# Message passing over 128 small graphs: blocks 2 to 14 ranked by edge count, a heavy and a light graph sharing nine slot tiles

## The chip, the core and the metric

One core of a Trainium2 chip runs the whole kernel. It has five engines that the profile names: PE (matrix products), DVE and ACT (vector and scalar work), POOL (vector work, and the queue that can issue indirect transfers) and SP (whose queue issues nearly all other transfers). Each works through its own queue in order; they wait for one another by semaphores. The metric is the device time in microseconds, the median of several runs.

## The reference

There are B = 128 graphs of N = 64 nodes with C = 128 features, in `x` (128, 64, 128), and a symmetric 0/1 matrix `adj` (128, 64, 64) with ones on the diagonal. The reference computes, for every ordered pair (i, j) of nodes of a graph, a message by a three-layer perceptron, keeps the messages whose `adj[i, j]` is 1, sums them over j, and feeds node i and its sum to a second perceptron:

```python
f_i, f_j = x[:, :, None, :], x[:, None, :, :]            # both broadcast to (B, P, P, C)
messages = mlp(concat(f_i, f_j), msg_*)                   # relu, layernorm, relu, layernorm, linear
agg      = sum(messages * adj[..., None], axis=2)
updated  = x + mlp(concat(x, agg), upd_*)
```

with `mlp` = linear, ReLU, layer normalization, linear, ReLU, layer normalization, linear. The adjacency is random: with the reference's seed a graph has 498 to 622 ones, 552 on average, of 4096.

## The kernel before, in words

Only the edges are computed. An edge gets a **slot**; a graph has CAP = 640 slots, which is five tiles of 128 (`TG = 5`). Two graphs make a **pair** (64 nodes on partitions 0 to 63, 64 on 64 to 127), four pairs a **block** of eight graphs, 16 blocks in all. All tiles are laid end to end and cut in **chunks** of four tiles (512 slots): 640 tiles, 160 chunks, ten a block. Weights that depend only on parameters are derived at the start.

For each block, `load_adj` and `load_x` bring the adjacency and the features (tiles `an`, `xn`), `rank` counts each node's edges along its row (`rk`), `count` sums the counts over nodes by a product with a triangular matrix (`lt`), `place` and `place_out` give every edge its slot number (`posall`), and `rows`, `rows_hi` and `rows_lo` make the first layer's two products for every node, split in a high and a low part (`abh`, `abl`).

For each pair, `distance` and `make_tp` (ACT, DVE) mark which slots belong to which node i (`tp`, 640 columns); `node_rows` casts it on POOL (`i`), `marks` and `compare` (PE, DVE) find node j of each slot (`j`), and `stack` puts both one above the other by four transfers on SP's queue into the 0/1 matrix `s`. `node_marks` turns `tp` by a transposing transfer (`oh`) for the sum at the end.

For each chunk, `gather` (L933) multiplies `s` by `abl` and `abh` into the PSUM bank `hps`, in pieces that end at a graph's border; `relu0` (ACT, L938) gives `h`; `turn_h` (PE, L943) transposes it four times for `stats0` (DVE, L629), the first normalization's sums. `layer1` (PE, L986) multiplies each of the four tiles by `w1c` into bank `z`. The bias, scaled by the deviation, is added in one of two ways, chosen by `by_vector`: for half of the chunks POOL makes it (`seed_all`, `u`, L973) and DVE adds it with the ReLU (L613); for the others ACT writes it into the bank first (`seed`, L980) and applies the ReLU (L997). `stats1` (DVE, L629) sums up the result `y`. For a group of five chunks `var1_step`, `root1_of` and `inverse_of` give the factors `m_q`; `weights` (POOL, L1029) multiplies them with `oh`, and `reduce` (PE, L1044) sums the slots of each node, after which a `Unit` runs the second perceptron for the block and `finish` stores 512 rows of the output.

The order is written by hand: `at(n, tag, fn, ...)` gives each step a time, 144 units a chunk plus a correction from the table `WHEN`, and a sort by these times is the order in which every engine's queue is filled. Nothing reorders it later. If a graph does not fit its slots, a flag sends all graphs through a dense path behind.

Of the kernel before, what the change touches and what calls it, by code (L numbers as in the profile page):

```python
# [25 lines left out]
    "<lambda>.3": {100: 398},  # L26
    "<lambda>.4": {100: 795},
    "<lambda>.6": {100: 4632},
    "<lambda>.7": {100: 284},
    "ahead.0": {100: 233},  # L30
    "ahead.1": {100: 132},
    "ahead.10": {100: 11},
    "ahead.11": {100: -1},
    "ahead.2": {100: 50},
    "ahead.5": {100: 113},
    "ahead.8": {100: 157},
    "ahead.9": {100: 215},
    "bias0": {3: -1471, 112: -1906, 113: -1642, 114: -17},
    "bias0_0": {115: 1153},
    "bias0_2": {115: 525},  # L40
    "bounds": {100: -15375},
# [8 lines left out]
    "count": {8: -190, 101: 140, 102: 122, 115: -186},  # L50
    "count.0": {100: 47},
    "count_out": {9: -228, 101: -2, 102: 190, 115: -239},
    "count_out.0": {100: 63},
    "degrees": {9: -358, 101: -137, 102: 105, 115: -608},
    "degrees.0": {100: -699},
    "distance": {0: -539, 3: 150, 5: -495, 8: -349, 103: 84, 104: 283, 105: -140, 106: 202,
        107: -511, 108: 189, 158: -852, 159: -528, 160: -749, 161: -525, 162: -737, 163: -1005},
    "distance.0": {100: 181},
    "distance.1": {101: 189},
    "distance.2": {102: 311},  # L60
    "empties.0": {100: 111},
    "empties.1": {100: 152},
    "empties.10": {100: 200},
    "empties.11": {100: 169},
    "empties.2": {100: -14},
    "empties.3": {100: 100},
    "empties.4": {100: 111},
    "empties.5": {100: 55},
    "empties.6": {100: -50},
    "empties.7": {100: -92},  # L70
    "empties.8": {100: -22},
    "empties.9": {100: 128},
    "finish": {8: 220, 110: 217, 111: 771, 112: 335, 113: -14, 114: 4865},
    "finish_0": {115: 6154},
    "finish_2": {115: 6519},
    "flag_in": {100: 118},
    "flag_max": {100: 160},
    "flag_out": {100: 377},
    "flag_sum": {100: 514},
    "flag_turn": {100: 45},  # L80
# [295 lines left out]
def tile_gnn(  # L376
# [9 lines left out]
    uw2: bass.AP, ub2: bass.AP,  # L386
    out: bass.AP,
):

# [1255 lines left out]
```

## Time and profile before

| what | value |
|---|---|
| median of the runs | 498.48 us (497.48 to 499.75, three runs) |
| profiled execution, first to last instruction | 497.9 us, no time of its own beside this span |
| PE, PEld busy | 486.0 us, 461.3 us |
| DVE busy | 465.2 us |
| ACT busy | 397.3 us |
| POOL busy | 348.4 us |
| SP's transfers, share of the 16 DMA engines | 55.9%, 62.36 MB |

The time of an execution is that of its slowest core, here the only one. A group's mean duration of a PE instruction is not its share of the engine's time, since the next one starts before it ends; the steps from start to start are in the timeline.

### The profile page before, as it was taken

Reading aid. Unit: us, or ns where it says so; the run is one execution under the profiler, and the core shown is the slowest. Engines: PE = TensorE matmul, PEld = TensorE weight load, DVE = VectorE, ACT = ScalarE, POOL = GpSimd, SP = SyncE. Lnnn points to the kernel's source line nnn. Section 1 sums busy time; section 2 is a strip of 40 time slices with the busy share of each in tenths; the row PEclk is TensorE's granted clock in tenths of the full one; section 3 lists DMA queues with packets and bytes.
Section 4 is the critical chain, followed back from the end, with each engine's and each line's share of the span. In section 5 each row is a group of like instructions: output and inputs, shape, how many; then the busy total and the mean of one; then the engine's idle time right before and its main releaser. Section 6 shows DMA issues by size and latency. Waiting matters only on the chain. (4 is left out here: it accounts for less than half of the span.)

```text
span 497.9 us, 15949 instructions
## 1 busy us (share of the span) xinstructions
PE 486.0 (98%) x5947; PEld 461.3 (93%) x5947; DVE 465.2 (93%) x1225; ACT 397.3 (80%) x907; POOL 348.4 (70%) x563
## 2 busy tenths in 40 slices
PE   7999999999999999999999999999999999999995
PEld 5889999999999999999899999999999999999994
DVE  7999999999999999999999999999999988989985
ACT  6999978878787887878778786888878778867754
POOL 3285776967959676795867859676696859565770
PEclk9999999999999999999999999999999999999998
DMA  4766836367574656854465574656655448625331
GB/s 122 148 145 157 182 99 150 93 167 152 126 140 110 126 142 150 168 122 118 117 143 143 126 153 103 132 128 158 152 123 128 101 112 165 152 74 129 66 34 47
DMA packets 91474, 63.55 MB, mean 128 GB/s; under 512 B 57473, under 2 KB 75522, under 8 KB 91394
## 3 DMA queue, kind: packets, MB, share of 16 engines
q1 hardware_dynamic: 91106, 62.36, 55.9%
q8 instruction: 49, 0.80, 0.7%
q14 instruction: 31, 0.25, 0.2%
q10 hardware_dynamic: 288, 0.13, 0.1%
HBM read 7.15 MB, written 4.19 MB: 23 GB/s over the span
## 5 line engine op out<-in xcount | busy, mean ns | idle before, releaser
L986 PE MATMUL z<-w1c,h 128*128 128x128 f32 x1280 | 190.0, 275 | 0.0
L986 PEld LDWEIGHTS z<-w1c,h 128*128 128x128 f32 x1280 | 172.4, 192 | 4.0 <-DVE uy_st L629 0.2
L938 ACT ACTIVATE h<-hps,b0c 128x512 f32<-128x512 f32 x160 | 109.0, 682 | 36.0 <-PE hps L933 35.5
L629 DVE BATCH_NORM_STATS2 st<-hT 128x6 f32<-128x256 f32 x320 | 122.9, 417 | 7.1 <-PE hT L943 4.8
L629 DVE BATCH_NORM_STATS2 st<-y 128x6 f32<-128x256 f32 x320 | 127.1, 419 | 0.5 <-ACT y L997 0.3
L980 ACT ACTIVATE z<-b1b,m_sd 128x128 f32<-128x128 f32 x320 | 117.3, 368 | 9.2 <-DVE y L613 3.6
L943 PE MATMUL hT<-ident,h 128*128 128x128 f32 x640 | 112.9, 276 | 0.3 <-DVE st L629 0.2
L933 PE MATMUL hps<-s,abl 128*128 128x512 f32 (+3 forms) x256 | 96.6, 380 | 2.6 <-ACT h L938 2.1
L933 PE MATMUL hps<-s,abh 128*128 128x512 f32 (+3 forms) x256 | 89.8, 358 | 0.0
L973 POOL TENSOR_TENSOR u<-b1b,m_sd 128x512 f32<-128x512 f32 x80 | 83.7, 1049 | 7.6 <-ACT m_sd L637 7.6
L943 PEld LDWEIGHTS hT<-ident,h 128*128 128x128 f32 x640 | 76.3, 141 | 3.4 <-issue 1.2
L1029 POOL TENSOR_TENSOR w<-oh,m_q 128x192 f32<-128x192 f16 x126 | 62.1, 514 | 9.4 <-DVE m_q L658 3.1
L916 DVE TENSOR_TENSOR j<-mk,cmpt 128x320 fp32r<-128x320 f32 x124 | 59.4, 479 | 6.3 <-PE mk L908 3.9
L891 POOL CAST i<-tp 128x640 fp32r<-128x640 f16 x58 | 41.8, 720 | 29.3 <-DMA s<-i 27.7
L997 ACT ACTIVATE y<-z 128x512 f32<-128x512 f32 x80 | 47.4, 595 | 17.8 <-PE z L986 17.5
L613 DVE CUSTOM_DVE_ANT_0 y<-z,u 128x512 f32<-128x512 f32 x80 | 54.1, 676 | 4.0 <-PE z L986 3.7
L933 PEld LDWEIGHTS hps<-s,abl 128*128 128x128 f32 x256 | 48.8, 191 | 8.0 <-ACT h L938 3.7
L876 ACT ACTIVATE d<-slot,mid 128x640 f16<-128x640 f16 x64 | 52.1, 818 | 1.7 <-POOL mid L765 1.0
L647 POOL TENSOR_TENSOR m_v<-m_v,st 128x20 f32<-128x20 f32 x31 | 7.3, 234 | 60.9 <-DVE st L629 59.6
L933 PEld LDWEIGHTS hps<-s,abh 128*128 128x128 f32 x256 | 49.1, 192 | 0.2
L1044 PE MATMUL ys<-y,w 128*32 128x128 f32 x1488 | 44.1, 274 | 0.0
L1044 PEld LDWEIGHTS ys<-y,w 128*32 128x32 f32 x1488 | 39.6, 110 | 2.5 <-issue 2.1
(193 smaller groups left out, 887.9 us busy)
## 6 DMA issues: line engine op xcount, KB each, us to landing
s<-i SPq DMA_DIRECT2D x124, 160.0 KB, 3.0
s<-j SPq DMA_DIRECT2D x124, 160.0 KB, 2.8
xn<-in_x_dram SPq DMA_DIRECT2D x15, 256.0 KB, 3.9
out_dram<-uo SPq DMA_DIRECT2D x15, 256.0 KB, 2.5
an<-in_adj_dram SPq DMA_DIRECT2D x16, 128.0 KB, 3.5
oh<-tp SPq DMA_TRANSPOSE x64, 3.0
xn<-in_x_dram SPq DMA_DIRECT2D x2, 128.0 KB, 3.0
out_dram<-uo SPq DMA_DIRECT2D x2, 128.0 KB, 3.4
```

The lines of the kernel that those rows point to most:

```text
L613: nc.vector._custom_dve(TENSOR_ADD_SAT, out=o, in0=ps, in1=sb, s0=BIG, s1=0.0)
L629: nc.vector.bn_stats(st, src.rearrange("p t c -> p c t"))
L876: nc.scalar.activation(D[p], slot.rearrange("p (t e) -> p t e", e=P), AF.Abs, bias=blocks[b]["mid"][:, q:q + 1], scale=-1.0)
L916: nc.vector.tensor_tensor(JR[p][:, c], MK.pop((p, k))[:, 0:HC], cmpt[:, c], op=ALU.is_equal)
L933: nc.tensor.matmul(HP[n][:, c:c + w], lhsT=blocks[g // (2 * PB)]["ab", g // 4 % 2][k][:, g % 4, :], rhs=S[g // 2][:, g % 2, e:e + w], star ...
L938: nc.scalar.activation(H[n], HP.pop(n), AF.Relu, bias=b0c)
L943: nc.tensor.transpose(HT[n][:, t, :], H[n][:, t * P:(t + 1) * P], ident)
L973: nc.gpsimd.tensor_tensor(U[n], bc(W["b1b"], CH), SR[q][:, k:k + CH].unsqueeze(2).to_broadcast([P, CH, C]), op=ALU.mult)
L980: nc.scalar.activation(z_of(n)[:, t, :], W["b1b"], AF.Copy, scale=SR[q][:, k:k + 1])
L986: nc.tensor.matmul(ps[:, t, :], lhsT=H[n][:, t * P:(t + 1) * P], rhs=W["w1c"], start=by_vector(n) and t == 0, stop=True, skip_group_check= ...
L1029: (nc.vector if p == NP - 2 else nc.gpsimd).tensor_tensor(WT[p][:, g], oh, qs, op=ALU.mult)
L1044: nc.tensor.matmul(YS[b][g * N + m * HN:g * N + (m + 1) * HN, k, :], lhsT=w[:, g, m, u, :], rhs=y, start=(u == 0), stop=(u == TH - 1), til ...
```

## The change

Blocks 0, 1 and 15 stay as they are. In blocks 2 to 14 (104 graphs) a pair gets nine tiles in place of ten. The pair's first graph fills slots from the front, the second from the back (`lts`, `lth` and `side` take the place of `lt` in `count`, `count_out` and `whole`), and they share the middle tile: the first may use slots 0 to 639 of 1152, the second 576 to 1151, and both are gathered into columns 576 to 639. A node's upper half still starts at slot 256 or later, counted from the graph's own end. So a block has nine chunks, and the program 147 chunks in place of 160, in 588 tiles in place of 640. The columns gathered for a pair fall from 1280 to 1216; everything that works on a pair's 640-column marks, on the block or on the second perceptron keeps its size. Of the nine chunks four go by POOL and DVE and five by ACT (before, five and five). The flag's test is extended by two columns for the new borders.

Which graphs meet is found on the chip. `all_adj` loads the 104 adjacency matrices once more, a graph a partition, by eight transfers of 104 x 512; `edges` adds the eight on POOL; `sort_keys` to `sort_out` rank the sums with a handful of DVE instructions and two products, and place the graph of rank r at position 2r or at the mirrored odd position, so that the heaviest meets the lightest. The list `idx` holds for each block of the 128 partitions' rows in `x`, `adj` and the output (a graph is 16 rows).

With it each of the 13 blocks is moved by way of memory: `fetch` gathers the adjacency (128 rows of 1 KB) and later the features (128 rows of 2 KB) by an indirect transfer on POOL's queue into `stg` (two buffers), `put` writes them to a scratch `far` on SP's queue, and `load_adj` and `load_x` read them from there; at the end `finish` stores to `far`, `take_out` reads it back and `send` scatters the rows to the output by an indirect transfer on POOL.

The core of the diff (the table `WHEN` is replaced whole: an absolute time for each step in place of corrections; `column`, `group_tiles` and `graph_tile` take the place of divisions by fixed sizes):

```diff
+    def tight(b):
+        return 2 <= b < NB - 1
+    TIGHT_TILES = 9
+    def graph_tile(g):
+        p = g // 2
+        return tile0[p] + (g % 2) * (CH if tight(p // PB) else TG)
...
-        yp = es.enter_context(tc.tile_pool(name="yp", bufs=19))
+        stg = es.enter_context(tc.tile_pool(name="stg", bufs=2))
+        far = es.enter_context(tc.tile_pool(name="far", bufs=1, space=bass.MemoryType.DRAM))
+        yp = es.enter_context(tc.tile_pool(name="yp", bufs=18))
...
         def at(n, tag, fn, *args):
-            t = WHEN.get(f"{fn.__name__}{tag}", {}).get(n % 10 if 14 <= n < 138 else 100 + v, 0)
-            plan.append((SCALE * n + t, len(plan), fn, args))
+            t = WHEN[base][k] if base in WHEN else SCALE * n
+            plan.append((t, len(plan), fn, args))
...
+        def fetch(what, b):
+            ap, n = rows_of[what]
+            st = STG[what, b] = stg.tile([P, N // SUB * C], F32, name="stg")
+            nc.gpsimd.indirect_dma_start(
+                st[:, 0:n], None, ap,
+                bass.IndirectOffsetOnAxis(ap=SORT["idx"][:, b - 2:b - 1], axis=0))
+        def put(what, b):
+            nc.sync.dma_start(far_of(what, b), STG.pop((what, b))[:, 0:rows_of[what][1]])
+        def take_out(b):
+            st = STG["o", b] = stg.tile([P, N // SUB * C], F32, name="stg")
+            nc.sync.dma_start(st, far_of("o", b))
+        def send(b):
+            nc.gpsimd.indirect_dma_start(
+                rows_of["o"][0], bass.IndirectOffsetOnAxis(ap=SORT["idx"][:, b - 2:b - 1], axis=0),
+                STG.pop(("o", b)), None)
+        def all_adj(k):
+            t = SORT["adj", k] = yp.tile([P, CH, C], F32, name="y")
+            nc.sync.dma_start(
+                t[0:NS].rearrange("p t c -> p (t c)"),
+                adj[S0:S1].rearrange("b i j -> b (i j)")[:, k * 512:(k + 1) * 512])
+        def edges(k):
+            nc.gpsimd.tensor_tensor(SORT["adj", 0][0:NS], SORT["adj", 0][0:NS],
+                                    SORT.pop(("adj", k))[0:NS], op=ALU.add)
...
         def pieces(n):
-            at_, end = n * CH * P, (n + 1) * CH * P
+            t0, b = CH * n, block_of[n]
+            lo, hi = t0 * P, (t0 + CH) * P
+            for g in range(2 * PB * b, 2 * PB * (b + 1)):
+                at_ = graph_tile(g) * P
+                skip = P // 2 if tight(b) and g % 2 else 0
+                a, z = max(lo, at_ + skip), min(hi, at_ + CAP)
+                if a < z:
+                    yield g, a - at_, a - lo, z - a
...
             r = (u.b * PB + u.k0) * P
+            if tight(u.b):
+                nc.sync.dma_start(graphs_of("o", u.b)[:, u.q, :], o)
+                return
...
-            return n % 10 in (1, 3, 6, 8, 9)
+            return n - chunk0[block_of[n]] in (1, 3, 6, 8, 9)
```

Three places of the new order. First POOL's queue at the start, from the slots of block 0 (`place_rest`) to the first scaled biases `u`. Before:

```order
L799 TENSOR_TENSOR pos<-rk,before 128x192
L804 TENSOR_TENSOR posall<-pos,an 64x3x64 x2
L749 TENSOR_SCALAR cumall<-raw 128x4
L763 TENSOR_TENSOR before<-cumall,deg 128x4
L765 TENSOR_TENSOR mid<-cumall,before 128x4
L767 TENSOR_TENSOR pos<-rk,before 128x256
L776 TENSOR_TENSOR posall<-pos,an 64x4x64 x2
L973 TENSOR_TENSOR u<-b1b,m_sd 128x512 x3
```

and now, from the slots of block 1 (`y` is here the loaded adjacency that `edges` adds, `stg` behind the two fetches the staging buffer):

```order
L1162 TENSOR_TENSOR pos<-rk,befall 128x256
L1171 TENSOR_TENSOR posall<-pos,an 64x4x64 x2
L1036 TENSOR_TENSOR y<-y 104x512 x7
L1373 TENSOR_TENSOR u<-b1b,m_sd 128x512 x2
L996 DMA stg<-in_adj_dram,idx 128x256 x2
L1258 CAST abh<-ab 128x512
L1259 TENSOR_TENSOR abl<-ab,abh 128x512
L1373 TENSOR_TENSOR u<-b1b,m_sd 128x512
```

The seven additions stand between block 1's slots and the first `u`, and the first two fetches right behind two of them.

Second SP's queue where the loads of the parameters end. Before:

```order
L453 DMA b0r<-in_L_gnn_msg_b_dram 1x128
L719 DMA an<-in_adj_dram 128x4x64 x2
L898 DMA s<-i_336 64x640 x2
L898 DMA s<-j_324 64x640
L1018 DMA_TRANSPOSE oh<-tp 128x5x128
```

and now:

```order
L685 DMA b0r<-in_L_gnn_msg_b_dram 1x128
L1030 DMA y<-in_adj_dram 104x512 x8
L1293 DMA s<-i_415 64x640
L1293 DMA s<-j_441 64x640 x2
L1293 DMA s<-i_415 64x640
```

Eight loads of the ranking stand ahead of the first stacked marks `s`, and the two loads of `an` (blocks 2 and 3) have gone from there.

Third SP's queue in a block of the middle, around the store of a block's result. Before:

```order
L1018 DMA_TRANSPOSE oh<-tp 128x5x128
L1162 DMA out_dram<-uo 128x4x128
L898 DMA s<-j_5557 64x640
L898 DMA s<-i_5589 64x640 x2
L898 DMA s<-i_5408 64x640
L898 DMA s<-j_5557 64x640
```

and now, with the adjacency of a later block read from `far` on the way:

```order
L1564 DMA far_o_4787<-uo 128x4x128
L1293 DMA s<-j_4582 64x640
L1293 DMA s<-i_4659 64x640
L1014 DMA an<-far_a_4593 128x4x64
L1293 DMA s<-j_4756 64x640
L1421 DMA_TRANSPOSE oh<-tp 128x5x128
L1293 DMA s<-i_4650 64x640 x2
L1293 DMA s<-j_4756 64x640
L1005 DMA stg<-far_o_4787 128x512
L1014 DMA an<-far_a_3914 128x4x64
```

The store goes to the scratch, and eight rows later the same bytes are read back; `s` transfers stand on both sides of that read.

More of the change, by code (lines that the diff above doesn't have):

```diff
@@ L50 @@
[L50 to L59, printed above, removed]
@@ L370 @@
-    "weights.1.1": {2: -269, 7: -112, 151: -490, 153: 294, 155: 117, 157: 234, 159: 279, 161: 259,
-        163: 359},
+    "<lambda>.3": (4012,),
+    "<lambda>.4": (220,),
+    "<lambda>.6": (2030,),
+    "<lambda>.7": (1181,),
+    "ahead.0": (47,),
+    "ahead.1": (43,),
+    "ahead.10": (113,),
+    "ahead.11": (142,),
+    "ahead.2": (84,),
+    "ahead.5": (100,),
+    "ahead.8": (131,),
+    "ahead.9": (121,),
+    "all_adj.0": (3,),
+    "all_adj.1": (8,),
+    "all_adj.2": (27,),
+    "all_adj.3": (35,),
@@ new lines @@
+    "all_adj.4": (44,),
+    "all_adj.5": (62,),
+    "all_adj.6": (114,),
+    "all_adj.7": (116,),
+    "bias0": (
+        4445, 4047, 3639, 3854, 3375, 2949, 2595, 2631, 2374, 1730, 1733, 1143, 501, 921, 429),
+    "bias0_0": (4254,),
+    "bias0_2": (4176,),
+    "bounds": (1004,),
[14 rows of a table added]
+    "count": (33, 358, 463, 656, 879, 1208, 1559, 1832, 2100, 2348, 2667, 2938, 3203, 3509, 3761),
+    "count.0": (2,),
+    "count_out": (
+        42, 360, 490, 665, 883, 1256, 1564, 1833, 2101, 2372, 2682, 2960, 3204, 3510, 3769),
@@ new lines @@
+    "odd_weights.0": (78,),
+    "ones": (951,),
+    "place": (61, 364, 584, 713, 1053, 1333, 1569, 1863, 2158, 2393, 2728, 2961, 3208, 3533, 3798),
+    "place_first": (7,),
+    "place_out": (
+        63, 382, 654, 799, 1144, 1475, 1696, 1996, 2224, 2430, 2816, 2984, 3278, 3632, 3862),
+    "place_pair.0": (13,),
+    "place_rest": (37,),
+    "put.a": (289, 272, 532, 693, 778, 959, 1545, 1745, 1467, 1889, 2242, 2904, 3087),
+    "put.x": (385, 434, 630, 764, 1009, 1298, 1731, 2091, 2145, 2545, 2744, 3245, 3584),
@@ L425, in tile_gnn, with column, group_tiles @@
     NP = B // 2
-    NQ = B // 4
-    QT = 4 * TG
     CH = 4
-    QC = QT // CH
-    NCHK = NQ * QC
     PB = 4
     NB = NP // PB
-    CPB = NCHK // NB
+    def tight(b):
+        return 2 <= b < NB - 1
+    S0, S1 = 2 * PB * 2, (NB - 1) * PB * 2
+    NS = S1 - S0
+    NF = 5
+    QC = 5
+    TIGHT_TILES = 9
+    tile0, chunk0, groups = [], [], []
+    for b in range(NB):
+        tiles = TIGHT_TILES if tight(b) else 2 * TG
+        chunk0.append(tile0[-1] // CH if tile0 else 0)
+        if tile0:
+            chunk0[-1] = (tile0[-1] + (TIGHT_TILES if tight(b - 1) else 2 * TG)) // CH
+        for q in range(PB):
+            tile0.append((tile0[-1] + (TIGHT_TILES if tight((len(tile0) - 1) // PB) else 2 * TG))
+                         if tile0 else 0)
+        chunks = tiles * PB // CH
+        groups += [(b, 0, 5), (b, 5, chunks)]
+    NCHK = (tile0[-1] + 2 * TG) // CH
+    NQ = len(groups)
+    block_of = [max(b for b in range(NB) if chunk0[b] <= n) for n in range(NCHK)]
+    group_of = [2 * b + (n - chunk0[b] >= 5) for n, b in enumerate(block_of)]
+    def column(n):
+        b, k0, _ = groups[group_of[n]]
+        return CH * (n - chunk0[b] - k0)
+    def group_tiles(q):
+        return CH * (groups[q][2] - groups[q][1])
+    def graph_tile(g):
+        p = g // 2
+        return tile0[p] + (g % 2) * (CH if tight(p // PB) else TG)
     updp = ctx.enter_context(tc.tile_pool(name="upd", bufs=1))
@@ new lines, in sort_keys @@
+        def sort_keys():
+            key = SORT["key"] = const.tile([P, 4], F32, name="key")
+            nc.vector.tensor_reduce(key[0:NS, 0:1],
+                                    SORT.pop(("adj", 0))[0:NS].rearrange("p t c -> p (t c)"),
+                                    axis=AX.X, op=ALU.add)
+            nc.vector.tensor_tensor(key[0:NS, 1:2], key[0:NS, 0:1], SORT["who"][0:NS, 0:1],
+                                    op=ALU.add)
+            d = SORT["diag"]
+            nc.vector.tensor_scalar(d[0:NS, 0:NS], ident[0:NS, 0:NS], key[0:NS, 1:2], float(C),
+                                    op0=ALU.mult, op1=ALU.mult)
@@ new lines, in sort_list, with sort_out @@
+        def sort_list():
+            ps = SORT["ps"] = abank()
+            d = SORT["diag"]
+            nc.tensor.matmul(ps[:, 0:NB - 3], lhsT=d[0:NS, 2 * P:3 * P], rhs=SORT["blk"][0:NS],
+                             start=True, stop=True)
+        def sort_out():
+            SORT["idx"] = const.tile([P, NB - 3], I32, name="idx")
+            nc.vector.tensor_scalar(SORT["idx"], SORT.pop("ps")[:, 0:NB - 3], SORT["who"][:, 2:3],
+                                    float(B * SUB - 1), op0=ALU.add, op1=ALU.min)
+            SORT.pop("diag")
@@ L1046, in reduce @@
                                          stop=(u == TH - 1), tile_position=(0, g * N + m * HN))
-            if p % 2:
-                for n in range(p // 2 * QC, (p // 2 + 1) * QC):
-                    del Y[n]
+            end = tile0[p + 1] if p + 1 < NP else NCHK * CH
+            for n in range(tile0[p] // CH, end // CH):
+                del Y[n]
         def reduce_block(b):
@@ L1256, in edge_path @@
                 at(n + t[14], v, finish, u)
+                if tight(b):
+                    at(n + t[14] + 2, "", take_out, b)
+                    at(n + t[14] + 4, "", send, b)
         for p in range(NP):
-            n = p * TG * 2 // CH
+            n = tile0[p] // CH
+            q = 2 * (p // PB) + p % PB // 2
+            end = chunk0[p // PB] + groups[q][2] + L1
+            last = q == NQ - 1
             if p > 1:
@@ L1340, in marks_here @@
         def marks_here(p):
-            S[p] = sp.tile([P, 2, CAP], F32R, name="s")
+            if p not in S:
+                S[p] = sp.tile([P, 2, CAP], F32R, name="s")
             marks(p, 0)
@@ L1346, in rows_here @@
         def rows_here(p, g):
+            if p not in S:
+                S[p] = sp.tile([P, 2, CAP], F32R, name="s")
             nc.scalar.copy(S[p][0:N, g, :], TP[p][g * N:(g + 1) * N])
```

525 lines of the change are left out of this document (340 added, 185 removed), and 598 rows, old and new, of the table WHEN.

## The prediction

> **What bounds the kernel now.** I read the page's first two lines, then the busy time by stretch, then who waited for whom.
>
> ```profile
> span 497.9 us, 15949 instructions
> PE 486.0 (98%) x5947; PEld 461.3 (93%) x5947; DVE 465.2 (93%) x1225; ACT 397.3 (80%) x907; POOL 348.4 (70%) x563
> ```
>
> In the stretches, the columns are the busy time of PE, PEld, DVE, ACT and POOL with the instructions in brackets, the granted clock, the share of the DMA engines and GB/s:
>
> ```profile
> 0.00:20.00 20.00, 16.67 (x134) 12.37 (x135) 16.61 (x46) 15.53 (x34) 7.27 (x21) 1.00 0.59 127
> 20.00:40.00 20.00, 19.54 (x209) 17.62 (x211) 18.04 (x47) 18.85 (x44) 12.83 (x17) 1.00 0.60 139
> 40.00:60.00 20.00, 19.73 (x207) 18.43 (x208) 19.64 (x53) 19.43 (x48) 11.85 (x24) 1.00 0.82 180
> 60.00:360.00 300.00, 298.46 (x3811) 287.84 (x3813) 287.98 (x747) 243.80 (x550) 224.86 (x357) 1.00 0.59 134
> ```
>
> From 60 to 360 us PE is busy for 298.5 of 300 us at a granted clock of 1.00, DVE for 288 (96%), ACT 81%, POOL 75%. Two engines are nearly full, so I ask which of them waits. Columns: us waited in total, times, the longest.
>
> ```profile
> POOL m_v L647 <- DVE st L629: 59.6, 18, 5.1
> ACT h L938 <- PE hps L933: 35.5, 54, 1.8
> POOL i L891 <- DMA s<-i: 27.7, 13, 3.7
> DVE st L629 <- PE hT L943: 4.8, 13, 1.0
> PEld hps L933 <- ACT h L938: 3.7, 7, 0.8
> ```
>
> The others wait for PE, and PE's longest entry is 3.7 us. PE is the bound, DVE close behind. A busy share says little of a pipelined PE, so I check its pace: do its instructions follow each other without a hole?
>
> ```profile
> 253.29 0.61 PE L986 MATMUL z<-w1c,h 128*128 128x128 f32 x4
> 253.74 0.60 PE L943 MATMUL hT<-ident,h 128*128 128x128 f32 x4
> 254.18 0.61 PE L986 MATMUL z<-w1c,h 128*128 128x128 f32 x4
> 254.62 0.30 PE L908 MATMUL mk<-tp,posall 128*128 128x320 f16 x1
> 257.11 0.48 PE L933 MATMUL hps<-s,abl 128*128 128x512 f32 x1
> 257.43 0.61 PE L1111 MATMUL mu<-u2c,uyT 128*128 128x128 f32 x4
> ```
>
> They do: four records of 128 columns take 0.44 to 0.45 us from start to start, 0.11 each, and a 512-column gather 0.32. These steps, not the mean durations, are what a removed instruction gives back on PE.
>
> **What leaves.** 52 tiles (640 less 588). The groups, with their number, busy time and mean duration in ns:
>
> ```profile
> L986 PE MATMUL z<-w1c,h 128*128 128x128 f32 x1280 | 190.0, 275 | 0.0
> L629 DVE BATCH_NORM_STATS2 st<-y 128x6 f32<-128x256 f32 x320 | 127.1, 419 | 0.5 <-ACT y L997 0.3
> L629 DVE BATCH_NORM_STATS2 st<-hT 128x6 f32<-128x256 f32 x320 | 122.9, 417 | 7.1 <-PE hT L943 4.8
> L973 POOL TENSOR_TENSOR u<-b1b,m_sd 128x512 f32<-128x512 f32 x80 | 83.7, 1049 | 7.6 <-ACT m_sd L637 7.6
> L613 DVE CUSTOM_DVE_ANT_0 y<-z,u 128x512 f32<-128x512 f32 x80 | 54.1, 676 | 4.0 <-PE z L986 3.7
> L933 PE MATMUL hps<-s,abl 128*128 128x512 f32 x64 | 30.6, 478 | 0.4 <-DVE abl L867 0.3
> L933 PE MATMUL hps<-s,abl 128*128 128x128 f32 x64 | 16.8, 263 | 0.0
> ```
>
> A tile has two records of `layer1` (1280 for 640 tiles) and one transpose: 3 x 0.11 = 0.335 us. A pair also gathers 64 columns fewer, twice (`abl`, `abh`): the two gather rows differ by 215 ns over 384 columns, 0.56 ns a column, so 0.07 us. Together 0.407 us, and 52 times that is **21.2 us off PE**. Bounds: 17 (52 x 0.335, the narrower gather for nothing) to 23 (gather at the whole 0.32/512 = 0.63 ns a column, 21.6, and with the 13 chunks some of the waits above).
>
> Is PE still the bound? DVE loses 26 sums of each kind (26 x 0.397 + 26 x 0.384 = 20.3 us by busy time) and 13 of L613 (8.8), 29 us: more than PE, so it doesn't take over. ACT loses 13 of `h`; five chunks of nine stay on it, and it has a fifth of its time free. Thirteen `u` leave POOL.
>
> **What is added in the middle.** Three indirect issues a block on POOL, which no row here shows. The nearest rows are the issue of a plain transfer on SP and a whole-tile instruction of POOL:
>
> ```profile
> 12.45 0.44 SPq L453 DMA_DIRECT2D ube1c<-in_L_gnn_upd_ln_b_dram  x1
> L1087 POOL TENSOR_TENSOR xo<-xn,cu2b 128x512 f32<-128x512 f32 x15 | 21.9, 1461 | 0.0
> ```
>
> So 0.44 to 1.46 us each; since POOL works through 128 rows for one, I take the `u` row's 1.05. How long is a block? The next block's `rk` is a block later:
>
> ```profile
> 240.86 0.67 DVE L731 TENSOR_TENSOR_SCAN rk<-first,an 128x256 f16<-128x256 f32 x1
> 270.70 0.68 DVE L731 TENSOR_TENSOR_SCAN rk<-first,an 128x256 f16<-128x256 f32 x1
> ```
>
> 29.84 us before, so 29.84 - 4 x 0.407 = 28.2 after. POOL has 224.86/300 x 29.84 = 22.4 us in a block; less one `u` and with a small step more, 21.6; with 3 x 1.05 it is 24.7 of 28.2 (88%), with 3 x 1.46 26.0 (92%). That fits beside PE, but with less slack than any engine but DVE and PE.
>
> On the transfers:
>
> ```profile
> q1 hardware_dynamic: 91106, 62.36, 55.9%
> xn<-in_x_dram SPq DMA_DIRECT2D x15, 256.0 KB, 3.9
> out_dram<-uo SPq DMA_DIRECT2D x15, 256.0 KB, 2.5
> ```
>
> A block moved 134 GB/s x 29.84 us = 4.0 MB. Now 128 and 256 KB are fetched and put, 256 KB taken back and sent: 1.28 MB more, 5.3 MB in 28.2 us, 187 GB/s and by the same price a byte a share of 0.82. The stretch from 40 to 60 us ran at just 180 GB/s and 0.82, with PE busy for 19.7 of 20 us; so I cost this at nothing, hidden behind PE. The chain fetch, put, load is three landings of 2.5 to 3.9 us, 12 us at most; the code asks for the fetch 25 chunks (some 75 us) ahead of the block. SP gets four more issues a block (0.44 to 0.6 us). The output's way back is waited for by nothing but the end of the run, and block 15, which ends last, stores directly.
>
> **What is added at the start.** Here the blocks' cover is missing: block 2 can't be loaded before the ranking, and the ranking stands in the queues.
>
> ```profile
> 13.63 1.09 SPq L719 DMA_DIRECT2D an<-in_adj_dram  x2
> 15.24 1.19 SPq L898 DMA_DIRECT2D s<-i  x2
> 17.23 1.61 POOL L776 TENSOR_TENSOR posall<-pos,an 64x256 f16<-64x256 f32 x2
> 24.72 3.04 POOL L973 TENSOR_TENSOR u<-b1b,m_sd 128x512 f32<-128x512 f32 x3 [5.89 <-ACT m_sd L637]
> 26.55 0.68 DVE L613 CUSTOM_DVE_ANT_0 y<-z,u 128x512 f32<-128x512 f32 x1
> ```
>
> Eight issues of 0.46 take the place of two: the first `s` goes out at 17.8 in place of 15.2 us. Behind them 1.7 MB move, at the stretches' 127 to 180 GB/s 9.5 to 13.4 us, so the last of them lands at 23 to 27 us. POOL is free of block 1's slots at 18.8; seven additions at 1.05 to 1.46 us end at 26.2 to 29.0. The `u` behind them, and the first `y`, started at 24.7 and 26.6. Behind the last addition DVE has about ten short ranking steps (nearest rows 0.17 to 0.6 us, some 3 us) with two products between, ahead of that `y`. So the first `y` moves to 29.5 to 32: 3 to 5.5 us late. What is queued behind it: all of DVE, and PE's next use of both `z` banks. Since PE's early `layer1`, transposes and gathers of chunk 5 and on are put elsewhere, some of it is filled; DVE at 18 of 20 us can't make up much. I take **4 us**, bounds 1 to 6, and below that nothing.
>
> **The sum.** 497.9 - 21.2 + 4 = 480.7. The median stands 0.6 over the profiled span, and 13 count products and the ranking's two add half a microsecond to PE: **482**. By the bounds: 498.5 - 23 + 1 = 476.5 to 498.5 - 17 + 6.5 = 488.
>
> **The rivals.**
> *POOL is held, and the kernel is slower.* POOL's queue is in order; an indirect issue waits for one of two staging buffers, which are free only when SP's `put` or POOL's own `send` has landed, and behind it stand `u`, `i` and `w`. For it: POOL already waits in order (59.6 and 27.7 us above), and each `put` stands in a queue with `s` transfers. It decides from the point where three issues with their waits exceed 28.2 - 21.6 = 6.6 us a block, 2.2 each. At 3 us each a block takes 30.6 us, 13 x 2.4 = 31 us more than forecast: 513. Against it: a buffer is held for two landings of 2.5 to 3.9 us, three times in a block, so for 24 of 56 buffer-microseconds at most.
> This rival has a page. The Trainium skill (SBUF — State Buffer, "A bandwidth-pool intuition that's wrong (but worth ruling out)") says that an issue from GpSimd needs the port that VectorE's two-port instructions lock, and took about 3100 ns in place of 620 beside such copies. By the higher figure the estimate would be 13 x (21.6 + 9.3 - 28.2) = 35 us on top of 482. What would lock it here is mainly `tp`:
>
> ```profile
> L882 DVE TENSOR_SCALAR tp<-d,deg 128x640 f16<-128x640 f16 x64 | 34.3, 535 | 0.5 <-ACT d L876 0.3
> ```
>
> That is 7% of the span, so the trace bears the rule out little.
> *The transfers crowd.* At a share of 0.82 the `s` transfers land later than 3 us, POOL's `i` waits longer than its 27.7 us, and PE misses `s` for a little in each block. For 0.8 us a block: 492. For: 13 such waits exist already. Against: the stretch at 0.82.
> *More than the sum.* The start hides the ranking, and DVE, 29 us lighter, closes PE's gaps: 498.5 - 23 - 1.5 = 474. For: DVE's relief is larger than PE's. Against: PE hardly waits for DVE in the waits above.
> *The change doesn't do what it says.* If a pair didn't fit 1152 slots, the flag would send all 128 graphs through 32 tiles each, 4096 tiles, milliseconds. By the reference's own inputs the ranked pairs have 1102 to 1120 edges and need at most 1134 slots with the gap at 256, so 0.01.
>
> **How the numbers follow.** Forecast (482, its own range 476.5 to 488) 0.60; held POOL 0.12; crowding (488 to 500) 0.17; more than the sum (470 to 476) 0.10; no fit 0.01. Half a per cent, 2.5 us, is about what a measurement tells from no change. Faster by more (under 496): 0.60 + 0.10 + 0.13 of crowding = 0.83. Within: 0.03 of crowding and 0.02 of held POOL = 0.05. Slower 0.12. The range leaves out most of held POOL, and the ends of crowding and of the last case: 473 to 497.
>
> **What would show it.** PE's busy share at 97% or more, 1176 records of L986's successor, a block of 28.2 us from `rk` to `rk`, DVE some 26 us lighter, the first `y` by DVE at 29 to 32 us. Wrong: a block of 29 us or more with PE waiting for `hps` or `z`; POOL above 95%, or rows where POOL waits on a staging buffer; `s` landing at 4 us or later; a start that lost over 8 us.

## The result, and the profile after

The changed kernel takes **574.87 us** (median of four runs, 572.43 to 579.22), the kernel before in the same comparison 498.24 (497.48 to 499.75): a ratio of **1.155, 95% interval 1.149 to 1.161**. It is 15.5% slower where 3% faster was forecast. The profiled execution spans 575.1 us.

The head of the page after (answering to the busy line shown of before):

```profile
span 575.1 us, 15718 instructions
PE 506.0 (88%) x5812; PEld 449.3 (78%) x5812; DVE 455.5 (79%) x1177; ACT 393.5 (68%) x907; POOL 392.4 (68%) x635
...
q1 hardware_dynamic: 97658, 72.58, 57.2%
q0 software_dynamic: 2704, 8.52, 5.4%
```

The work did leave. DVE has 455.5 us in place of 465.2: its two groups of sums and the `y` of `by_vector` lose 22.9 us, the rest of its busy time is 13.2 us longer. The groups have the counts that the prediction worked out:

```profile
L1385 PE MATMUL z<-w1c,h 128*128 128x128 f32 x1176 | 170.5, 279 | 8.0 <-ACT z L1379 6.4
L882 DVE BATCH_NORM_STATS2 st<-hT 128x6 f32<-128x256 f32 x294 | 119.2, 422 | 65.2 <-PE hT L1344 58.9
L1344 PE MATMUL hT<-ident,h 128*128 128x128 f32 x588 | 128.4, 284 | 41.7 <-DVE st L882 40.8
```

1176 records of `layer1` are 1280 less 104, and 588 transposes 640 less 52. But read the last column, the idle time just before the group and what ended it. PE and DVE each name the other: DVE's sums wait 58.9 us for PE's transposes (4.8 before), and PE's transposes 40.8 us for DVE's sums. No engine is full any more. The waits of after, longest first (us in total, times, longest):

```profile
ACT h L1339 <- PE hps L1333: 65.2, 70, 3.9
DVE st L882 <- PE hT L1344: 58.9, 88, 4.1
PEld hT L1344 <- DVE st L882: 52.0, 62, 2.2
PE hT L1344 <- DVE st L882: 40.8, 64, 2.4
...
POOL u L1373 <- ACT m_sd L890: 24.8, 12, 6.6
...
POOL i L1286 <- DMA s<-i: 5.2, 4, 2.5
```

Before, the fourth of these read:

```profile
PE hT L943 <- DVE st L629: 0.2, 1, 0.2
```

What is not in the list matters too: POOL waits less for `s` transfers than before (5.2 us, 27.7 before), and nothing there waits for a staging buffer. In the middle of the run PE works 277 of 300 us; the first row, of the start, shows a granted clock of 0.83, where before had 1.00:

```profile
20.00:40.00 20.00, 13.27 (x70) 9.80 (x70) 13.12 (x36) 7.33 (x17) 9.30 (x8) 0.83 0.40 97
...
100.00:400.00 300.00, 276.75 (x3270) 250.62 (x3270) 251.11 (x635) 215.82 (x495) 223.69 (x357) 0.99 0.71 157
```

To see where the 77.2 us between the two spans arise, I cut each run at two rows of DVE: the last step of the second perceptron, `uo`, for block 0 and for block 10. First before, then after:

```profile
113.07 1.12 DVE L1159 SCALAR_TENSOR_TENSOR uo<-mu,um_q,xo 128x128 f32<-128x128 f32 x4
413.77 1.11 DVE L1159 SCALAR_TENSOR_TENSOR uo<-mu,um_q,xo 128x128 f32<-128x128 f32 x4
```

```profile
155.34 1.11 DVE L1560 SCALAR_TENSOR_TENSOR uo<-mu,um_q,xo 128x128 f32<-128x128 f32 x4
481.75 1.11 DVE L1560 SCALAR_TENSOR_TENSOR uo<-mu,um_q,xo 128x128 f32<-128x128 f32 x4
```

The start is 42.3 us longer, the ten blocks between are 32.64 us each in place of 30.07 (25.7 together), the end 9.2 us longer (93.3 for 84.1). The forecast was 4 us at the start and 1.63 us *less* a block.

### The profile page after: what moved, and what is told of

Same layout as the page of the kernel before. It is cut to its first block, busy times and chain, and to the rows that moved or that the text cites. A ratio compares the mean times of both kernels' runs of the same rounds, so it can differ in the third digit from the quotient of the medians.

```text
span 575.1 us, 15718 instructions
## 1 busy us (share of the span) xinstructions
PE 506.0 (88%) x5812; PEld 449.3 (78%) x5812; DVE 455.5 (79%) x1177; ACT 393.5 (68%) x907; POOL 392.4 (68%) x635
## 4 chain that ended last, share of the span: by engine, by line
## 5 line engine op out<-in xcount | busy, mean ns | idle before, releaser
L1385 PE MATMUL z<-w1c,h 128*128 128x128 f32 x1176 | 170.5, 279 | 8.0 <-ACT z L1379 6.4
L882 DVE BATCH_NORM_STATS2 st<-hT 128x6 f32<-128x256 f32 x294 | 119.2, 422 | 65.2 <-PE hT L1344 58.9
L1344 PE MATMUL hT<-ident,h 128*128 128x128 f32 x588 | 128.4, 284 | 41.7 <-DVE st L882 40.8
L1385 PEld LDWEIGHTS z<-w1c,h 128*128 128x128 f32 x1176 | 152.8, 193 | 13.9 <-ACT z L1379 9.9
L1339 ACT ACTIVATE h<-hps,b0c 128x512 f32<-128x512 f32 x147 | 100.5, 684 | 68.9 <-PE hps L1333 65.2
L1379 ACT ACTIVATE z<-b1b,m_sd 128x128 f32<-128x128 f32 x320 | 117.0, 369 | 23.9 <-PE z L1385 16.9
L882 DVE BATCH_NORM_STATS2 st<-y 128x6 f32<-128x256 f32 x294 | 116.4, 417 | 3.6 <-ACT y L1396 3.1
L1333 PE MATMUL hps<-s,abl 128*128 128x384 f32 (+7 forms) x256 | 92.7, 376 | 3.8 <-issue 2.2
L1373 POOL TENSOR_TENSOR u<-b1b,m_sd 128x512 f32<-128x512 f32 x67 | 69.9, 1047 | 25.0 <-ACT m_sd L890 24.8
L1333 PE MATMUL hps<-s,abh 128*128 128x512 f32 (+7 forms) x256 | 84.3, 350 | 0.0
L864 DVE CUSTOM_DVE_ANT_0 y<-z,u 128x512 f32<-128x512 f32 x67 | 45.6, 680 | 12.6 <-PE z L1385 9.7
L1303 PE MATMUL mk<-tp,posall 128*128 128x320 f16 x126 | 38.9, 308 | 0.8 <-DVE j L1311 0.4
```

The costliest lines, as they stand in the source:

```text
L882: nc.vector.bn_stats(st, src.rearrange("p t c -> p c t"))
L1333: nc.tensor.matmul(HP[n][:, c:c + w], lhsT=blocks[g // (2 * PB)]["ab", g // 4 % 2][k][:, g % 4, :], rhs=S[g // 2][:, g % 2, e:e + w], star ...
L1339: nc.scalar.activation(H[n], HP.pop(n), AF.Relu, bias=b0c)
L1344: nc.tensor.transpose(HT[n][:, t, :], H[n][:, t * P:(t + 1) * P], ident)
L1373: nc.gpsimd.tensor_tensor(U[n], bc(W["b1b"], CH), SR[q][:, k:k + CH].unsqueeze(2).to_broadcast([P, CH, C]), op=ALU.mult)
L1379: nc.scalar.activation(z_of(n)[:, t, :], W["b1b"], AF.Copy, scale=SR[q][:, k:k + 1])
```

## The experiments

Thirteen kernels ran. This table cuts the main ones in the same way (us; the block is the distance of the two `uo` rows over ten; the end runs from the second to the span's end; medians are of four or five runs, and 498.0 to 498.7 for the kernel before beside them):

| kernel | median | ratio to before, 95% | first `uo` | a block | end |
|---|---|---|---|---|---|
| before | 498.2 | | 113.1 | 30.07 | 84.1 |
| the change | 574.9 | 1.149 to 1.161 | 155.3 | 32.64 | 93.3 |
| the change, sums behind the turns | 541.3 | 1.081 to 1.088 | 144.8 | 30.86 | 87.7 |
| the change, no way by memory | 564.6 | 1.128 to 1.136 | 152.4 | 32.26 | 90.7 |
| both of these | 532.8 | 1.064 to 1.074 | 141.1 | 30.43 | 87.2 |
| new table | 536.9 | 1.070 to 1.083 | 138.7 | 29.87 | 98.1 |
| new table, ranking kept, no way by memory | 524.1 | 1.049 to 1.057 | 136.2 | 29.43 | 91.9 |
| new table, neither | 514.4 | 1.028 to 1.040 | 125.8 | 29.17 | 91.6 |
| table for late landings | 523.5 | 1.047 to 1.055 | 137.4 | 28.62 | 98.5 |
| before, sums ahead of a turn | 562.4 | 1.125 to 1.131 | 129.1 | 33.64 | 95.2 |

My theory after reading the two traces: the new order puts work in one another's way on a shared bank. The rivals: the transfers and the ranking cost it, or the nine-tile layout itself is worse.

### The old order, and the new order without the change

The first attempt took the order back. The change with a table carried over from the order before, each step at the place that its like had there:

```diff
-    WHEN = {... a place of its own for each step ...}
+    WHEN = {... the places of the order before, nine chunks a block, the ranking's steps added ...}
```

> The changed kernel with all its parts (nine tiles, ranking, transfers by way of memory), but its table of times is made from the order of the kernel before: each step of a block stands where its counterpart stood there, chunk c of nine at the place of chunk 10c/9 of ten; the new transfers stand 4 us of that order ahead of their use. Theory 'order' (the new table alone loses the time, PE and DVE alternate over one PSUM bank): 478 to 500 us, and DVE's and PE's waits for each other over hT fall from 40 to 59 us each to under 15. Theory 'transfers' (the way through memory holds queues): 560 us or more, since every transfer is still there. Theory 'layout' (nine tiles in uneven chunks and groups suit no order): 550 us or more.

Measured: **664.64 us** (ratio 1.330 to 1.342). And the same without ranking and transfers:

```diff
-    WHEN = {...}                                   # as above
...
         def put(what, b):
-            nc.sync.dma_start(far_of(what, b), STG.pop((what, b))[:, 0:rows_of[what][1]])
+            pass
...
-            nc.sync.dma_start(an, graphs_of("a", b) if tight(b) else
-                              adjp[:, b * PB:(b + 1) * PB, :])
+            nc.sync.dma_start(an, adjp[:, b * PB:(b + 1) * PB, :])
...
```

`fetch`, `take_out`, `send` and the steps of the ranking are emptied like `put`, and the features and the results go straight as the adjacency does.

> Both edits together: the order made from that of the kernel before, and no ranking and no way by memory (the same part of the result left out as in the run without it). What is left of the change are the nine tiles. Theory 'order': 473 to 490 us, the 21 us that the 52 tiles cost PE come off 498 where the order suits. Theory 'transfers': 475 to 490, and then the run with the order alone is slow. Theory 'layout': 550 or more.

Measured: **614.96 us** (1.231 to 1.237). Then the other way round, the ten-tile kernel of before with its steps at the places that the new table gives them, stretched to ten chunks a block:

```diff
-    WHEN = {... corrections to 144 units a chunk ...}
+    WHEN = {... the change's places, read off at nine tenths of a chunk's number ...}
```

> The kernel before, ten tiles and direct loads, computing all of the result, but its steps in the order of the changed kernel: each step of a block stands where its counterpart stands in the new table, chunk c of ten at the place of chunk 9c/10. Theory 'order': 560 to 610 us, far above 498, though nothing of the nine tiles or of the transfers is in it. Theories 'transfers' and 'layout': 495 to 515.

Measured: **699.96 us** (1.400 to 1.408), with all of before's work. All three lie above what the theory 'order' expected, by 165, 125 and 90 us. The first two lie where the rival 'layout' put them (550 or more), the first also where 'transfers' did. They don't tell which part of the change costs what: an order carried over by position may suit neither layout, so the layout is asked again below with orders made for it. They do show the size of the thing that the prediction had at nothing: the same instructions take 498 or 700 us by order alone.

They also give one clean reading of the start, since the first two begin in before's order. The first `y` of DVE, without and with the ranking:

```profile
26.74 0.68 DVE L569 CUSTOM_DVE_ANT_0 y<-z,u 128x512 f32<-128x512 f32 x1
```

```profile
32.65 0.69 DVE L569 CUSTOM_DVE_ANT_0 y<-z,u 128x512 f32<-128x512 f32 x1
```

26.55 before, so up to this row the layout costs the start nothing (0.2 us), and the ranking, with the transfers that follow it, 5.9 us.

### The shared bank

Where do PE and DVE wait for each other? `hT` is one bank of PSUM for a chunk: PE's four transposes fill its quarters, DVE's two sums read its halves. The timeline of after at the start, PE and DVE alone:

```profile
20.74 0.76 DVE L882 BATCH_NORM_STATS2 st<-hT 128x6 f32<-128x256 f32 x2
21.65 0.30 PE L1344 MATMUL hT<-ident,h 128*128 128x128 f32 x1 [2.44 <-DVE st L882]
...
22.01 0.27 PE L1344 MATMUL hT<-ident,h 128*128 128x128 f32 x1
22.32 0.43 DVE L882 BATCH_NORM_STATS2 st<-hT 128x6 f32<-128x256 f32 x1 [0.43 <-PE hT L1344]
22.81 0.33 PE L1344 MATMUL hT<-ident,h 128*128 128x128 f32 x1 [0.52 <-DVE st L882]
...
23.20 0.42 PE L1344 MATMUL hT<-ident,h 128*128 128x128 f32 x1
23.85 0.42 DVE L882 BATCH_NORM_STATS2 st<-hT 128x6 f32<-128x256 f32 x1
```

Follow one chunk from 21.65, where its first transpose has waited 2.44 us for the sums of the chunk before (there is one `hT`): two transposes, then the sum of these two, and only then the third transpose, which stood still 0.52 us "<-DVE st", then the fourth and the second sum. The third transpose writes other columns than the sum reads, but waits for it. The order asks for this: in the program of the change the first half's sum is queued ahead of the chunk's last transpose in 72 of 146 chunks (and in chunk 0, which is ordered apart), in the program before in none of 159. The Trainium skill (PSUM — Partial Sum Buffer, "PSUM bank collisions raise a hardware error ⚠️") says that two engines must not touch one bank at a time, at different columns either, so that a semaphore has to stand between them; the trace shows the wait at that place, 0.52 us here. One rule was added to the change (`seeded` has no use in it):

```diff
+        turned, seeded = {}, {}
+        for t, _, fn, args in plan:
+            if fn is turn_h:
+                turned[args[0]] = max(turned.get(args[0], t), t)
+            if fn is seed:
+                seeded[args[0]] = max(seeded.get(args[0], t), t)
+        plan = [(max(t, turned[args[0]] + 0.5) if fn is stats0 else t, k, fn, args)
+                for t, k, fn, args in plan]
         for _, _, fn, args in sorted(plan, key=lambda v: v[:2]):
```

> The changed kernel with one rule more on its order: the first half of the sums over hT (two of a chunk's four tiles) never stands ahead of the chunk's last transposes. In the new order it does so in 72 of the 146 chunks that take this way, in 38 of them ahead of both last transposes; in the order before in none. Both touch the one PSUM bank hT, so PE stands still until DVE has read it, and only then turns the rest. Theory 'shared bank' (this place of the order is the main loss): PE's and PEld's waits for st over hT fall from 41 and 52 us to under 20 each, and the time by 30 to 50 us, to 525 to 545. Theory 'whole order' (the raggedness of the table as a whole): under 10 us, 565 or more, the waits move to other rows.

Measured: **541.30 us** (539.6 to 542.66), 33.6 less, or 0.47 us for each of the 72 places. PE's wait fell as it should; DVE's fell by 8.4 us only, since a chunk's sums still wait for its transposes:

```profile
DVE st L882 <- PE hT L1344: 50.5, 62, 3.0
...
PE hT L1344 <- DVE st L882: 12.1, 18, 1.9
```

The converse, on the kernel before: the same fault put into a good order, with nothing else changed than the place of these sums:

```diff
+        turned = {args: t for t, _, fn, args in plan if fn is turn_h}
+        plan = [(turned[args[0], 2] - 0.5 if fn is stats0 and args[1] == 0 and args[0] % 2 else t,
+                 k, fn, args) for t, k, fn, args in plan]
```

> The kernel before, ten tiles, direct loads, its own order, and one edit: in every second chunk (80 of 159) the first half of the sums over hT is queued ahead of the chunk's third transpose. Theory 'shared bank': each such chunk stops PE for the 0.84 us that PEld waits on average at that place in the changed kernel (52.0 us in 62 waits), 80 times 0.84 = 67 us, so 550 to 580 us, with PE and PEld waiting for st. Theory 'whole order': within 5 us of 498, for nothing else is moved.

Measured: **562.44 us**, 63.7 more than before, or 0.80 us for each of the 80 sums, nearly the whole of the wait on the path:

```profile
PEld hT L943 <- DVE st L629: 65.5, 80, 1.9
DVE st L629 <- PE hT L943: 62.9, 118, 1.7
...
PE hT L943 <- DVE st L629: 48.5, 80, 1.6
```

Eighty waits for eighty changed places. This cause is shown from both sides. The price is not a constant: 0.80 us in an order whose PE has no holes, 0.47 in the change's.

### The way by memory, and the ranking

The change's own order without ranking and transfers (the functions emptied as above):

> The changed kernel in its own new order, but the ranking, the indirect transfers and the scratch in memory are left out: blocks 2 to 14 are loaded and stored directly, graphs 2p and 2p+1 share nine tiles as they come (where they have too many edges for it some are lost, and the flag is held at zero), so all work on the engines behind the loading is the same. Theory 'order': 550 to 575 us, only the 12 us of the start may come back. Theory 'transfers': 480 to 500. Theory 'layout': 550 or more.

Measured: **564.62 us**, 10.3 less than the change. The same on top of the rule for the sums:

> The order of the change with the rule that the first half of a chunk's sums stands behind its last transpose (541.3 us), and without the ranking and the way by memory: natural pairs straight from x and adj, results stored straight to the output, the flag held at 0. What it leaves out: the choice of which graphs meet, and edges beyond a pair's slots. Theory 'the two costs add up': the way by memory cost 10 us in the change's own order, so 529 to 534 here. Theory 'the way by memory is hidden behind the waits for the shared bank': with those gone it costs more, as with the new table (22.6 us), so 516 to 522. Either way it stays over 498, since the rest of the order's waits (the z banks, the start) is still there; below 500 would say that these two causes are the whole loss.

Measured: **532.76 us**, 8.5 less than 541.30. So the two costs add up: 33.6 and 8.5 to 10.3. Even with both gone the kernel is 35 us over before.

Is the rest the layout, or the order still? I made a new table by list scheduling (each engine's steps placed in turn, the earliest due first), the sums behind all four transposes and `layer1` behind all four seeds:

```diff
-    WHEN = {...}
+    WHEN = {... another place for each step; nothing else ...}
```

> The changed kernel, all parts of it, computing everything, with another table of times and nothing else: a list made engine by engine, earliest due step first, with three rules: sums over hT behind all four transposes of the chunk, layer1 behind all four of the chunk's scaled biases, no step ahead of what it needs. Theory 'order' (it alone lost the time): 480 to 500 us, PE busy for 97% from 80 us on and a block of 27.5 to 28.5 us, as the removed tiles have it. Theory 'layout' or 'transfers': 540 us or more whatever the table says.

Measured: **536.94 us**, between the two theories, so neither held. And that table with neither ranking nor transfers, then with the ranking alone:

> The table of the run with the new table, without ranking, indirect transfers and scratch (blocks 2 to 14 loaded and stored directly, graphs 2p and 2p+1 sharing nine tiles as they come, edges without a slot lost, flag held at zero). The difference to the run with the new table is what the way by memory and the ranking cost in an order that suits: Theory 'order': 5 to 15 us less than that run, all of it in the first 60 us and the last 20. Theory 'transfers': 30 us less or more.

Measured: **514.39 us**, 22.6 less than with both: again between the two theories. Nine tiles in this order take 29.17 us a block, less than before's 30.07 (29.14 and 29.68 over the first nine steps alone), so in the blocks the layout as such is not worse.

> The new table of 536.9 us; the ranking is still worked out (eight loads, seven additions, the ranks), but blocks 2 to 14 are natural pairs straight from x and adj, stored straight to the output, the flag held at 0: only the fetches, puts, reads back and scatters are left out. What it leaves out: the use of the list. With both left out it was 514.4. Theory 'the start pays, for the ranking': 526 to 530, 12 to 16 us for the ranking and 7 to 11 for the transfers. Theory 'the way by memory pays': 514 to 519, nearly all of the 22.6 us for fetches that block 2 waits for and for transfers that crowd.

Measured: **524.09 us**. So with this table the ranking costs 9.7 us, all at the start (the first `uo` moves from 125.8 to 136.2), and the transfers 12.8 more: 2.5 at the start, 0.43 in each of ten blocks, 6.2 at the end. Neither theory's range was met (526 to 530, 514 to 519): the ranking and the transfers share the cost. What the transfers do in the blocks is seen in the same stretch with and without them (100 to 400 us; the last three columns are the clock, the share of the transfer engines and GB/s):

```profile
100.00:400.00 300.00, 290.13 (x3588) 272.18 (x3587) 266.12 (x696) 235.32 (x543) 243.19 (x389) 1.00 0.78 170
```

```profile
100.00:400.00 300.00, 293.18 (x3627) 276.36 (x3626) 272.43 (x706) 239.79 (x554) 222.35 (x370) 1.00 0.68 135
```

At a share of 0.78 PE loses 3 us in 300. POOL waits at the scatters, not for a free buffer as the first rival said but for the read back and, once, for a store; with the new table:

```profile
POOL out_dram L713 <- DMA stg<-far_o: 10.4, 6, 3.2
POOL out_dram L713 <- DMA out_dram<-uo: 8.8, 1, 8.8
```

The second row is most of the loss at the end. The last scatter stands behind block 15's direct stores and waits for them, though it writes other rows, and starts at 530.2 of 535.5 us. From the end of the last `uo` to the end of the span are 9.4 us, 4.6 without the transfers. The change itself sends that scatter ahead of the stores, and there it is 4.9.

If landings are late, an order can count on it. A second table, made in the same way, did:

> The change with a second new table, made like the one of 536.9 us but counting on transfers that land later, so that fetches, reads back and stacked marks stand earlier ahead of their use. Theory 'the way by memory costs because landings come later than the order counts on': 505 to 522. Theory 'it costs because of what it takes of POOL, SP and the transfer engines, wherever it stands': 530 to 540. Theory 'a nine-tile order can beat the ten-tile one': below 496.

Measured: **523.47 us**, 1.5 above the first theory's range, 13.5 better with all the transfers in. POOL's wait for `s` fell from 14.4 to 2.0 us. Its middle has a PE as full as the prediction had forecast for the change:

```profile
100.00:400.00 300.00, 297.79 (x3740) 281.45 (x3738) 274.64 (x716) 247.05 (x564) 252.50 (x400) 0.99 0.77 173
```

PE is busy for 297.8 of 300 us at 173 GB/s and a share of 0.77, POOL at 84%, and a block takes 28.62 us, 1.45 less than before. That difference leans on the cut: the tenth step of before, from the `uo` row at 380.23 to that at 413.77, is 33.5 us long. Over the nine steps ahead of it a block takes 29.68 us before and 28.69 here, 0.99 less. What is left of the loss stands at the start (24.4 us) and, by the cut of the table, the end (14.4); 8.9 us pass behind the last `uo` here, 4.5 before, since the last scatter again waits for the stores.

### The start

PE's granted clock drops there. The change's rows by 4 us (PE's busy time first, the clock third from the end):

```profile
16.00:20.00 4.00, 2.30 (x16) 1.68 (x14) 3.88 (x8) 3.95 (x8) 1.68 (x2) 1.00 0.71 219
20.00:24.00 4.00, 1.83 (x8) 1.11 (x8) 2.85 (x8) 2.06 (x6) 3.76 (x4) 0.88 0.70 193
24.00:28.00 4.00, 2.75 (x11) 1.79 (x10) 2.74 (x8) 1.31 (x4) 3.50 (x3) 0.50 0.73 164
```

The order before has products that nobody reads (`keep_busy`) to fill such holes. I put more of them where the kernel of 541.3 us has its holes:

```diff
+        for t, k in ((85.5, 10), (100.5, 14), (118.5, 8)):
+            plan.append((t, len(plan), keep_busy, (k,)))
```

> The kernel of 541.3 us (the change with the sums behind the turns), and 32 products of 128 columns that nobody reads, put on PE ahead of the first transposes of chunks 1, 2 and 3, where PE stood idle for 1.2, 1.7 and 0.9 us. Its granted clock there was 0.53, 0.50, 0.50 and 0.76 in the four stretches of 4 us from 20 us on, with PE busy for 12.1 of these 16 us. Theory 'the order's gaps at the start cost twice, since PE runs at half its clock after them': the clock stays at 1.00, some 5 us of PE come back, the first uo moves from 144.8 to 138 to 141 us, and the time is 534 to 538. Theory 'the start waits for DVE, ACT and POOL, and PE's clock is covered': the clock comes back, the first uo stays within 1.5 us, and the time is 539.5 to 543.

Measured: **543.95 us**, 1 us above the second theory's range, and the first `uo` at 143.5 in place of 144.8. The clock came back; this row read 0.50 without the fillers:

```profile
24.00:28.00 4.00, 3.65 (x31) 3.21 (x30) 3.29 (x10) 2.33 (x7) 3.76 (x4) 1.00 0.60 137
```

So in this kernel PE's half clock is a sign of the holes and not what the time is lost to. In the better table the ranking's additions hold POOL's queue:

```profile
19.50 2.63 POOL L741 TENSOR_TENSOR y<-y 104x512 f32<-104x512 f32 x2 [9.37 <-DMA y<-in_adj_dram]
```

```diff
-    "edges.1": (112,), "edges.2": (90,), "edges.3": (78,), "edges.4": (146,),
-    "edges.5": (61,), "edges.6": (136,), "edges.7": (68,),
+    "edges.1": (125.5,), "edges.2": (125.4,), "edges.3": (125.3,), "edges.4": (125.7,),
+    "edges.5": (125.1,), "edges.6": (125.6,), "edges.7": (125.2,),
```

> The table of 523.5 us, with the seven additions of the ranking on POOL moved behind block 1's slots. There POOL stood for 9.4 us waiting for one of the eight loads, with block 1's slots queued behind it; ACT's marks waited for these, and PE stood idle from 23.9 to 28.9 us and then ran at a granted clock of 0.50 to 0.72 for 8 us. Theory 'POOL's queue, held by the loads, makes the start late': the first uo moves from 137.4 to 130 to 134 us, and the time is 516 to 520. Theory 'the ranking is late next': the additions end as much later as they stand later, block 2 waits for the list, and the time stays at 521 to 526.

Measured: **523.48 us** (519.0 to 524.9), the same as without the edit. The additions now run behind block 1's slots, 9.4 us in one piece, and hold the casts of block 1's products in their stead. It is what the second theory's range said, though block 2's fetch comes no later for it (44.9 us, 45.4 without the edit). The profiled execution, at 519.0 us the quickest of the five (its span is 517.3), has its first `uo` at 133.9, and a hole of PE in another place:

```profile
32.00:36.00 4.00, 0.00 (x0) 0.00 (x0) 2.82 (x6) 0.00 (x0) 2.90 (x3) 0.58 0.27 45
```

One wait gave way to another. No version here beats the kernel before.

## Why the prediction was wrong

**The step that failed** is the sentence "These steps, not the mean durations, are what a removed instruction gives back on PE." It holds in an order in which PE has no holes, and that was read from the trace of *before*. The table `WHEN` was replaced whole. The prediction looked at what the new order does at three places, all of them added work, and took the rest at nothing. So the sum's main term, 21.2 us off, was credited to a PE that in the changed kernel is busy for 88%. Beside it, "The others wait for PE" was read too widely: of the rows shown that holds for ACT and DVE, while POOL's two long waits are for DVE and for a transfer.

**The term that is missing** is the shared bank `hT`, 33.6 us. The fault was to be read before the run, though not its price: the program's order shows for the queues of PE and DVE that a sum stands ahead of the third or fourth transpose of its own chunk, and the waits of before show PE held by it just once (0.2 us). Order says whether two engines touch a bank in turn; the trace says what a turn costs.

**The tiles.** The removed work was counted right. What it gives back where the order lets it count depends on the cut: 1.45 us a block with the second table is 0.36 us a tile, inside the bounds of 0.33 to 0.44 around the sum's 0.407; over nine steps it is 0.99, or 0.25 a tile, below them. In the change itself a block was 2.57 us longer.

**Transfers at nothing, "hidden behind PE".** Half wrong. In the blocks the stretch at 0.82 that the prediction went by was a fair guide: 0.43 us a block with the one table, and PE at 297.8 of 300 us at 0.77 with the other. The output's way back was said to be waited for by "nothing but the end of the run"; with the new table the transfers cost 6.2 us at the end, most of it one scatter's wait for block 15's stores. The rival "the transfers crowd" (0.8 us a block) had about twice the price, and its mechanism isn't shown: POOL's `i` waits for `s` 14.4 us with the transfers and 14.1 without. What the 0.43 us wait for stays open.

**The start.** "I take 4 us" for the ranking: 5.9 us at the first `y` where the order at the start was before's, 10.4 at the first `uo` with the new table. The first `y` of the change is at 39.2 us, for 29.5 to 32 predicted. But without the ranking and the transfers it is at 37.2, so 2.0 of the 12.7 us are theirs. The layout costs nothing up to this row, so the rest is the order.

**POOL.** Three issues a block at 1.05 us: right. The groups of after:

```profile
L1008 POOL DMA_INDIRECT out_dram<-stg,idx x13 | 13.8, 1063 | 3.1 <-issue 1.7 <-DMA oh<-tp 0.8 <-DVE um_q L913 0.5
L996 POOL DMA_INDIRECT stg<-in_adj_dram,idx x13 | 13.5, 1037 | 6.4 <-DVE idx L1104 4.1 <-issue 1.4 <-POOL posall L1171 0.3
L996 POOL DMA_INDIRECT stg<-in_x_dram,idx x13 | 13.2, 1013 | 2.7 <-issue 2.0
L1036 POOL TENSOR_TENSOR y<-y 104x512 f32<-104x512 f32 x7 | 8.9, 1278 | 3.5 <-DMA y<-in_adj_dram 3.0
```

The rival "POOL is held" forecast a slower kernel and had the sign right for a wrong reason: POOL is at 68%, and the longer issue that the Trainium skill (SBUF — State Buffer, "A bandwidth-pool intuition that's wrong (but worth ruling out)") gives beside VectorE's copies, 3100 ns, is not seen: the seven of the 39 issues that ran beside a `tp` took 951 to 1076 ns. The measurement decides.

**The other rivals.** "More than the sum" and "the change doesn't do what it says" can be dropped. The rival that came true, an order that makes two engines take turns, was not on the list, and so 497 could stand as the upper end.

**What stays open.** Of the 93 us between 482 and 575, 33.6 are the bank, 8.5 to 10.3 the ranking and the transfers, in the change's own order. Of the 50 that remain, some 18 are shown to be the rest of that order: with the same work in other tables 532.8 us become 514.4, and 541.3 become 523.5. Some 16 are the saving that didn't come (482 for 498), and 16 what the new table without ranking and transfers takes beyond before; whether order or layout loses these wasn't separated. Most of it stands at the start: with both causes gone the first `uo` of the change is still 28 us late. That a better order exists is shown (28.62 us a block), not that one exists which also starts and ends as early as before's. Which of the start's waits is the last one wasn't found: giving PE its clock back didn't move it, and moving the additions put another wait in place of theirs.

## What to carry to other kernels

Where a change replaces the order, price the order first: for each buffer with one copy that two engines share, ask of both queues who is ahead of whom, before and after, and what one turn costs by the trace. A saving per instruction, read from a trace without holes, is worth that much only in an order without holes; add the removed work as an upper bound and let the range reach to the order's worst. And when a large change disappoints, put the suspected fault alone into the good kernel: eighty changed places there cost 0.80 us each, near the mean wait of 0.84 read from the changed kernel, and nothing else had moved that could have cost it.

## What the runs showed of the hardware

PE's granted clock fell to a half without any long pause. In the kernel with the sums behind the turns the longest two holes between 16 and 22 us are 1.16 and 1.66 us, and yet:

```profile
16.00:20.00 4.00, 2.50 (x16) 2.01 (x16) 3.56 (x10) 3.95 (x7) 1.87 (x2) 1.00 0.81 253
20.00:24.00 4.00, 2.21 (x8) 1.63 (x8) 2.39 (x7) 2.42 (x6) 3.77 (x4) 0.53 0.45 150
24.00:28.00 4.00, 3.06 (x13) 2.53 (x14) 2.94 (x9) 1.48 (x4) 3.33 (x3) 0.50 0.69 157
```

The row at 63% busy is followed by one at 0.53. The Trainium skill (TensorE: Matmul & The Clock Gate, "What's actually happening") ties the fall to an idle window of some 3.4 us; here no hole was half as long. The clock's records in these traces last whole multiples of 3.41 us, the last of a run apart. Cut on that grid, the fifteen traces (without the last 15 us of each) show 41 falls, each at the end of a stretch with PE busy for at most 57%. Every stretch at 44% or less was followed by a fall; between these shares some were and some weren't (in this kernel 48% from 16.9 us was, 45% from 33.9 us wasn't). So in these rows the fall goes with the busy share of such a stretch, and not with one long hole. No run was made to test that.
